# Adding layer outputs to the image by accumulating DMA instead of VectorE, in a four-layer image kernel

## The chip, the core and the metric

One core of a Trainium2 chip runs the kernel. Its engines each work through their own queue of instructions: TensorE (PE in the profile, its weight loads PEld), VectorE (DVE), ScalarE (ACT), GpSimd (POOL) and SyncE (SP), which here only issues DMAs. All data is float32. The metric is device time in microseconds, the median of several runs of the whole program.

## The reference

Four images `x[b]` of 256 channels and 64 x 64 pixels pass through four layers. Each layer normalises the image by groups, computes something from it and adds the result to the image.

```
x = x + L0(gn(x))   # xs = relu(gn1(conv3x3(x)));  attention over all 4096 pixels, y = softmax(theta^T phi) g
                    # L0 = 0.1 * gn2(w y) + xs
x = x + L1(gn(x))   # linear attention, 4 heads; output rms-normalised over channels
x = x + L2(gn(x))   # depthwise 3x3 and pointwise 1x1 convolution, weights generated from the image, + bias
x = x + L3(gn(x))   # 1x1 convolution with a mixture of 4 experts, mixed by the pooled image
```

Here `gn` is the plain group normalisation over 32 groups (8 channels each). A layer's group statistics need the whole image after the layer before.

## The kernel before

The 256 channels are two halves `h` of 128 partitions, and an image is `big[128, 2, 4096]`. `xp` is a padded copy of the image, `tpg` holds theta, phi and g of the attention. The rest are small buffers: `k4` (ten tiles of 128x1024, shared by all helpers), `k2` (six of 128x512) and `bank` (eight PSUM banks).

The helpers are Python generators. `convolve` (L306) is layer 0's 3x3 convolution; it ends by writing xs to DRAM (`xs_d`, L411). `project` and `attend` (L434) compute the attention; one turn of `attend` is one block of 256 by 512 logits. `tail` (L833) runs the rest for an image: `nonlocal_out` (L490, the end of layer 0), `linear_attention` (L541), `generated` (L675) and `mixed` (L776). Every `yield n` of these says how many turns of the partner the work just written is worth. `Chain` (L39) sums these values times a rate and gives one turn for each whole unit; `w.later(n, f)` has `f` written n turns later. Inside `manual_schedule` each engine's order is the order in which the turns write instructions.

The order of the work: convolution and projection of image 0; then, for b = 0 to 2, attention of image b interleaved with the tail of image b-1 and the convolution of image b+1 (rate 1.5 for b = 0, else 0.8), and the projection of image b+1. The end is written so:

```
attention, before = attend(B - 1), Chain(tail(B - 2, big, qT), 2.0).steps()
run(attention, before)
spare = ...
last = Chain(tail(B - 1, tpg[:, 0:NH, :], tpg[:, NH, :], in_turns(spare, k4))).steps()
run(last, before, before)
run(before)
```

So attention of image 3 runs with the tail of image 2 beside it, and what is left of that tail runs beside the tail of image 3, whose image lies in `tpg`. The first argument of `run` takes one turn, and each further argument takes one turn after it.

The additions that the change touches are all on VectorE: in `nonlocal_out` a chunk of xs and one of x are loaded (L517, L518), and two `scalar_tensor_tensor` on 128x1024 form the sum (L531, L533); in `linear_attention` L657 adds a scaled PSUM bank to the image; in `generated` L745 adds the pointwise product and the bias; in `mixed` L829 adds product and image into `res`, which L830 stores to `out`. After each of the first three, `bn_stats` reads the new chunk. The depthwise convolution is 8 `scalar_tensor_tensor` per half chunk (L760, "taps" below), 64 per image; the centre tap is ScalarE's (`centre`, L729), and the first half chunk has 8 more on VectorE that form the pointwise weights `pk` (L764). In the profile most VectorE operations carry the lines of two helpers: L93 (`tt`) and L96 (`stt`); the tile names tell them apart.

Of the kernel before, what the change touches and what calls it, by code (L numbers as in the profile page):

```python
# [38 lines left out]
class Chain:  # L39
# [5 lines left out]

    def later(self, n, f):

        self.due.append((max([n] + [k for k, _ in self.due]), f))

    def pending(self):  # L50
        while self.due:
# [2 lines left out]
    def steps(self):  # L54
        credit = 0.0
        for part in (self.layers, self.pending()):
            for n in part:
                credit += n * self.rate
                while credit >= 1:
                    credit -= 1  # L60
                    yield
                    self.due = [(k - 1, f) for k, f in self.due]
                    while self.due and self.due[0][0] <= 0:
                        self.due.pop(0)[1]()


@with_exitstack
def conv_preact_fast(ctx: ExitStack, tc: tile.TileContext, guard, x, wc, wtpg, ww, wqkv, wout, w1cat, wd2,
# [11 lines left out]
    def k4(name):  # L80
        return wk.tile([P, CH], F32, tag="k4", name=name, bufs=10)

    def k2(name):
        return wk.tile([P, 512], F32, tag="k2", name=name, bufs=6)

# [8 lines left out]

    def stt(o, a, s, b, op0, op1):
        nc.vector.scalar_tensor_tensor(o, a, s, b, op0, op1)  # L96


    xp = cp.tile([P, NH, HW + 2, HW], F32, name="xp")
# [123 lines left out]
    def stats_tile():  # L223
        return sp.tile([P, NH, 8, 6], F32, name="st")
# [80 lines left out]

    def convolve(w, b):  # L306

        st = stats_tile()
        for h in range(NH):
            for c in range(8):  # L310
# [81 lines left out]
        for i, (a, k) in enumerate(PRODUCTS):  # L392
            if k == 1:
                for op, *args in down(a):
                    op(*args)
                    yield 0.25
            v, u = across(k), us
            if i + 1 < len(PRODUCTS):
                us = load_filters(i + 1)
            w.later(1, lambda a=a, k=k, v=v, u=u: products(a, k, v, u))  # L400
            yield 0.9
        yield from w.pending()
        stats(3)
        bias = vec_s[:, V_SB, :]
# [2 lines left out]
        for c in range(N // CH):  # L407
            cols = bass.ts(c, CH)
            for h in range(NH):
                nc.scalar.activation(big[:, h, cols], big[:, h, cols], AF.Relu, bias=sh[:, h:h + 1], scale=sc[:, h:h + 1])  # L410
                w.later(1, lambda h=h, cols=cols: nc.sync.dma_start(out=xs_d[b, h, :, cols], in_=big[:, h, cols]))  # L411
                yield 0.3


# [75 lines left out]
    def nonlocal_out(w, b, big, k4):  # L490

        st = stats_tile()

        def load_y(c):
            yt = k4("yl")
            nc.sync.dma_start(out=yt, in_=y_d[b, :, bass.ts(c, CH)])
            return yt

        ys = [load_y(0), load_y(1)]
        for c in range(N // 512):  # L500
            cols = bass.ts(c, 512)
            if c % 2 == 0 and c // 2 + 2 < N // CH:
                ys.append(load_y(c // 2 + 2))
            for h in range(NH):
                ps = bank("ps_wy")
                nc.tensor.matmul(ps, ww_s[:, bass.ts(h, P)], ys[c // 2][:, bass.ts(c % 2, 512)], start=True, stop=True)  # L506
                nc.scalar.copy(big[:, h, cols], ps)
# [4 lines left out]
        PARTS = [(c, h) for c in range(N // CH) for h in range(NH)]  # L512

        def load_parts(i):
            c, h = PARTS[i]
            xs, xr = k4("xs"), k4("xr")
            nc.sync.dma_start(out=xs, in_=xs_d[b, h, :, bass.ts(c, CH)])  # L517
            nc.sync.dma_start(out=xr, in_=x[b, bass.ts(h, P), bass.ts(c, CH)])  # L518
            return xs, xr

        parts = [load_parts(0), load_parts(1)]
# [4 lines left out]
        for i, (c, h) in enumerate(PARTS):  # L526
            cols = bass.ts(c, CH)
            if i + 2 < len(PARTS):
                parts.append(load_parts(i + 2))
            xs, xr = parts[i]  # L530
            stt(xs, big[:, h, cols], sc[:, h:h + 1], xs, ALU.mult, ALU.add)  # L531
            yield 0.7
            stt(big[:, h, cols], xs, sh[:, h:h + 1], xr, ALU.add, ALU.add)  # L533
            yield 0.7
            for s in range(2):
                nc.vector.bn_stats(st[:, h, 2 * c + s, :], big[:, h, bass.ts(2 * c + s, 512)])
            yield 0.5
        return st


    def linear_attention(w, b, big, qT, k4, st):  # L541
# [108 lines left out]

        def added(c, z):
            cols = bass.ts(c, 512)
            for h in range(NH):
                pt = bank("ps_zt")
                for j in range(4):
                    nc.tensor.transpose(pt[:, bass.ts(j, P)], z[:, j, bass.ts(h, P)], ident)
                stt(big[:, h, cols], pt, gains[:, 1, h:h + 1], big[:, h, cols], ALU.mult, ALU.add)  # L657
                nc.vector.bn_stats(st[:, h, c, :], big[:, h, cols])

        last = None  # L660
        for c in range(NC):
            zb = outputs(c)
            yield 0.6
            if last is not None:
                added(c - 1, last)
            last = scaled(*zb)
            yield 0.6
        yield 1
        added(NC - 1, last)
        return st  # L670


# [2 lines left out]
    def generated(w, b, big, k4, st):  # L675
# [13 lines left out]
        nc.sync.dma_start(out=pk, in_=bp2)  # L689

        def load_wp2(j):
            t = k4("wp2").rearrange("p (r o) -> p r o", r=2)
            nc.sync.dma_start(out=t, in_=wp2[:, bass.ts(j, 2), :])
            return t

# [34 lines left out]
            return t  # L730

        def pointwise(c, s, dw):
            res = []
            for oh in range(NH):
                ps = bank("ps_pw")
                for h in range(NH):
                    nc.tensor.matmul(ps, pk[:, h * NH * P + oh * P:h * NH * P + (oh + 1) * P], dw[h][:, bass.ts(s, 512)],  # L737
                                     start=(h == 0), stop=(h == NH - 1))
                res.append(ps)
            w.later(1, lambda: pointwise_added(2 * c + s, res))  # L740

        def pointwise_added(c, res):
            cols = bass.ts(c, 512)
            for oh in range(NH):
                stt(big[:, oh, cols], res[oh], vec_s[:, V_L2B, oh:oh + 1], big[:, oh, cols], ALU.add, ALU.add)  # L745
                nc.vector.bn_stats(st[:, oh, c, :], big[:, oh, cols])

        ahead = centre(0)
        slices = [load_wp2(0), load_wp2(1)]
# [26 lines left out]
    def mixed(w, b, big, k4, st):  # L776
        ex = []
        for j in range(NE // 2):
            ex.append(k4("ex").rearrange("p (k o) -> p k o", k=2))
# [41 lines left out]
        nc.vector.tensor_copy(b3, pb3[:, 0:NH])  # L821
        for c in range(N // 512):
            cols = bass.ts(c, 512)
            for oh in range(NH):
                ps = bank("ps_ex")
                for h in range(NH):
                    nc.tensor.matmul(ps, wm[:, h, bass.ts(oh, P)], big[:, h, cols], start=(h == 0), stop=(h == NH - 1))  # L827
                res = k2("res")
                stt(res, ps, b3[:, oh:oh + 1], big[:, oh, cols], ALU.subtract, ALU.add)  # L829
                w.later(1, lambda oh=oh, cols=cols, res=res: nc.sync.dma_start(out=out[b, bass.ts(oh, P), cols], in_=res))  # L830
                yield 0.1

    def tail(b, big, qT, k4=k4):  # L833
        def layers(w):
# [637 lines left out]
```

## Time and profile before

| | |
|---|---|
| median of 3 runs | 3421.85 us (3421.0 to 3424.05) |
| the profiled execution | 3416.84 us |
| its span, first to last instruction | 3413.4 us |
| mean granted TensorE clock | 0.954 |
| TensorE busy | 3054.3 us, 89% of the span |
| VectorE busy | 2180.1 us, 64% |
| ScalarE busy | 1140.2 us, 33% |
| GpSimd busy | 96.4 us, 3% |
| DMA | 151.18 MB, mean 44 GB/s, all issued by SP |

A profile shows one execution. The page's slices cut the span into 40 equal parts of 85 us; a digit is the busy share in tenths. A group is one line, engine and shape: its instructions, their busy time and mean duration in ns, then how long the engine was idle just before them and which engine's instruction ended that. A busy TensorE can be one at a lowered clock; the granted clock stands beside it in the windows.

### The profile page before, as it was taken

To read this page: it belongs to the slowest core of one execution; us is meant where nothing else is said; L and a number is where in the kernel's file an instruction comes from. 1 tells how busy PE (TensorE), PEld (TensorE's weight loads), DVE (VectorE), ACT (ScalarE), POOL (GpSimd) and SP (SyncE) were. 2 spreads that over 40 slices of the span, in tenths; PEclk is the share of its full clock that TensorE was granted. 3 is DMA by queue.
4 is the path that set the end of the run, shared out by engine and by line. 5 is a ranking of instruction groups with operands and counts; after the bars stand their busy time and mean duration, and the time that the engine had idled before them with its cause. 6 is when DMAs were issued, how large, how long until landed. Compare 5 with 4: busy or idle time off the path is not lost.

```text
span 3413.4 us, 23977 instructions
## 1 busy us (share of the span) xinstructions
PE 3054.3 (89%) x8322; PEld 1470.1 (43%) x8322; DVE 2180.1 (64%) x2689; ACT 1140.2 (33%) x2115; POOL 96.4 (3%) x133
## 2 busy tenths in 40 slices
PE   3699999999999999999999999999999999738736
PEld 1254434445454444435454444445445553315412
DVE  8836674434636987873726996883653464794585
ACT  2033224333445322223445322213435434314210
POOL 0000000000000000000001000000000010000100
PEclk9899999999999999999999999999999999968867
DMA  5310001002101011112200011112200000210201
GB/s 197 100 50 23 30 25 53 6 4 81 49 0 31 4 68 68 40 46 88 67 1 25 9 65 59 41 33 77 77 28 3 4 7 31 77 49 13 77 12 50
DMA packets 78721, 151.18 MB, mean 44 GB/s; under 512 B 8320, under 2 KB 45952, under 8 KB 76416
## 3 DMA queue, kind: packets, MB, share of 16 engines
q1 hardware_dynamic: 78592, 149.56, 12.8%
q8 instruction: 68, 1.11, 0.1%
q14 instruction: 61, 0.50, 0.0%
HBM read 101.30 MB, written 48.23 MB: 44 GB/s over the span
## 4 chain that ended last, share of the span: by engine, by line
PE 71%; DVE 24%; issue 2%; ACT 2%; DMA 1%; POOL 0%; SPq 0%; DVEq 0%; ACTq 0%; POOLq 0%
PE pf L443 20%; PE py L473 19%; PE ps_conv L347 9%; DVE dw L96 6%; PE ps_qkv L574 5%; PE ps_tp L422 3%; PE ps_ex L827 3%; DVE tot L93 3%; DVE big L96 2%; PE ps_pw L737 2%; PE ps_wy L506 2%; PE ps_g L427 2%; PE ps_h L699 1%; PE ps_o L637 1%; DVE inv L457 1%
## 5 line engine op out<-in xcount | busy, mean ns | idle before, releaser
L444 ACT ACTIVATE pr<-pf 128x512 f32<-128x512 f32 x1024 | 602.3, 595 | 1221.4 <-PE pf L443 1173.3
L443 PE MATMUL pf<-tpg 128*128 128x512 f32 x2048 | 972.8, 597 | 5.8 <-DVE inv L457 3.5
L473 PE MATMUL py<-pr,tpg 128*128 128x512 f32 x2048 | 964.0, 593 | 7.1 <-ACT pr L444 7.1
L93 DVE TENSOR_TENSOR tot<-tot,pr 128x1024 f32<-128x1024 f32 x448 | 546.3, 1219 | 308.3 <-ACT pr L444 305.5
L473 PEld LDWEIGHTS py<-pr,tpg 128*128 128x128 f32 x2048 | 389.8, 191 | 500.0 <-issue 475.9
L443 PEld LDWEIGHTS pf<-tpg 128*128 128x128 f32 x2048 | 382.2, 191 | 457.4 <-issue 425.6
L347 PE MATMUL ps_conv<-v,u 128*128 128x512 f32 x768 | 354.9, 613 | 51.2 <-DVE v L93 28.2
L96 DVE SCALAR_TENSOR_TENSOR dw<-xp,dk,dw 128x1008 f32<-128x1008 f32 x224 | 283.5, 1267 | 7.1 <-ACT dw L729 3.6
L347 PEld LDWEIGHTS ps_conv<-v,u 128*128 128x128 f32 x768 | 150.1, 197 | 246.9 <-issue 206.3
L737 PE MATMUL ps_pw<-dw,pk 128*128 128x512 f32 x224 | 115.6, 650 | 66.8 <-DVE dw L96 66.8
L582 DVE TENSOR_REDUCE qs<-qk 128x16 f32<-128x512 f32 x24 | 16.5, 686 | 186.6 <-ACT qk L576 186.6
L574 PE MATMUL ps_qkv<-wqkv_s,xg 128*128 128x384 f32 x384 | 134.5, 498 | 0.0
L422 PE MATMUL ps_tp<-big,wtpg_s 128*128 128x512 f32 x256 | 117.7, 603 | 2.9 <-ACT big L410 2.9
L93 DVE TENSOR_TENSOR v<-ra 128x1024 f32<-128x1024 f32 x96 | 115.3, 1218 | 0.4
L93 DVE TENSOR_TENSOR tpg<-ps_g,bg_s 128x512 f32<-128x512 f32 x32 | 22.1, 691 | 144.9 <-PE ps_g L427 144.9
L457 DVE RECIPROCAL inv<-pss 128x512 f32<-128x512 f32 x32 | 107.3, 3352 | 7.2 <-PE pss L455 7.2
L737 PEld LDWEIGHTS ps_pw<-dw,pk 128*128 128x128 f32 x224 | 45.0, 208 | 131.8 <-DVE dw L96 71.3
L574 PEld LDWEIGHTS ps_qkv<-wqkv_s,xg 128*128 128x128 f32 x384 | 73.7, 197 | 51.0 <-issue 12.1
L171 POOL TENSOR_TENSOR rstd<-rstd,half 128x2 f32<-128x2 f32 x24 | 16.7, 697 | 2627.4 <-DVE rstd L247 2090.5
L423 ACT ACTIVATE tpg<-ps_tp,btp_s 128x512 f32<-128x512 f32 x64 | 43.8, 686 | 123.0 <-PE ps_tp L422 123.0
L576 ACT ACTIVATE qk<-ps_qkv,rinv 128x256 f32<-128x256 f32 x96 | 45.4, 473 | 116.6 <-PE ps_qkv L574 115.0
L827 PE MATMUL ps_ex<-big,wm 128*128 128x512 f32 x192 | 84.0, 593 | 0.0
(238 smaller groups left out, 2756.0 us busy)
## 6 DMA issues: line engine op xcount, KB each, us to landing
u<-filters SPq DMA_DIRECT2D x192, 128.0 KB, 2.3
xp<-in_x_dram SPq DMA_DIRECT2D x16, 1024.0 KB, 5.3
xs_d<-big SPq DMA_DIRECT2D x32, 512.0 KB, 2.8
xr<-in_x_dram SPq DMA_DIRECT2D x32, 512.0 KB, 4.5
out_dram<-res SPq DMA_DIRECT2D x64, 256.0 KB, 2.0
xs<-xs_d SPq DMA_DIRECT2D x24, 512.0 KB, 4.1
y_d<-yt SPq DMA_DIRECT2D x32, 256.0 KB, 2.0
yl<-y_d SPq DMA_DIRECT2D x14, 512.0 KB, 5.7
```

The lines of the kernel that those rows point to most:

```text
L93: nc.vector.tensor_tensor(o, a, b, op)
L96: nc.vector.scalar_tensor_tensor(o, a, s, b, op0, op1)
L347: nc.tensor.matmul(ps[oh], u[oh][:, h, :], v[:, bass.ts(h, 512)], start=(h == 0), stop=(h == NH - 1))
L422: nc.tensor.matmul(ps, wtpg_s[:, h, k, :], big[:, h, cols], start=(h == 0), stop=(h == NH - 1))
L427: nc.tensor.matmul(ps[:, j, :], big[:, h, bass.ts(4 * c + j, P)], wtpg_s[:, h, 2, :], start=(h == 0), stop=(h == NH - 1))
L443: nc.tensor.matmul(pf, phi[:, bass.ts(2 * m + s, P)], theta[:, bass.ts(q, 512)], start=True, stop=True)
L444: nc.scalar.activation(pr[:, bass.ts(s, 512)], pf, AF.Exp)
L457: nc.vector.reciprocal(inv, pss)
L473: nc.tensor.matmul(py, g[:, bass.ts(2 * m + s, P)], probs[i][:, bass.ts(s, 512)], start=(m == 0 and s == 0), stop=(m == NM - 1 and s == 1))
L574: nc.tensor.matmul(ps[:, 0:3 * HID], xg[:, h, bass.ts(j, P)], wqkv_s[:, h, :], start=(h == 0), stop=(h == NH - 1))
L737: nc.tensor.matmul(ps, pk[:, h * NH * P + oh * P:h * NH * P + (oh + 1) * P], dw[h][:, bass.ts(s, 512)], start=(h == 0), stop=(h == NH - 1))
L827: nc.tensor.matmul(ps, wm[:, h, bass.ts(oh, P)], big[:, h, cols], start=(h == 0), stop=(h == NH - 1))
```

## The change

Five sums become accumulating DMAs issued from GpSimd, `add_by_dma`. ScalarE first writes the term into an SBUF tile (or scales it in place in layer 0), and the DMA adds it to its destination. In layer 0, `xs_d` is filled with x before the convolution, xs is added to it in DRAM, and the sum is later added to the scaled output in SBUF; the loads of xs and x by chunk go. `bn_stats` of a chunk is written two turns after its DMA (one in layer 0). In layer 3 the sum is formed in the image and stored from there. `pool4` is the same allocator as `k4`, also where `k4` is handed in as alternating with spare tiles. `later` no longer keeps the order of earlier entries. Some yields change, and in the end phase the rate of image 2's tail is 3.0 with three turns per turn of the last tail.

```diff
 class Chain:
     def later(self, n, f):
-        self.due.append((max([n] + [k for k, _ in self.due]), f))
+        self.due.append((n, f))
...
+    def add_by_dma(o, i):
+        nc.gpsimd.dma_start(out=o, in_=i, accum_op=ALU.add)
...
     def convolve(w, b):
+        for h in range(NH):
+            nc.sync.dma_start(out=xs_d[b, h], in_=x[b, bass.ts(h, P), :])
...
-                    yield 0.25
+                    yield 0.3
...
-            yield 0.9
+            yield 1.1
...
-                w.later(1, lambda h=h, cols=cols: nc.sync.dma_start(out=xs_d[b, h, :, cols], in_=big[:, h, cols]))
+                w.later(1, lambda h=h, cols=cols: add_by_dma(xs_d[b, h, :, cols], big[:, h, cols]))
...  nonlocal_out
-            xs, xr = parts[i]
-            stt(xs, big[:, h, cols], sc[:, h:h + 1], xs, ALU.mult, ALU.add)
-            yield 0.7
-            stt(big[:, h, cols], xs, sh[:, h:h + 1], xr, ALU.add, ALU.add)
-            yield 0.7
-            for s in range(2):
-                nc.vector.bn_stats(st[:, h, 2 * c + s, :], big[:, h, bass.ts(2 * c + s, 512)])
-            yield 0.5
+                nc.scalar.activation(big[:, h, cols], big[:, h, cols], AF.Identity, bias=sh[:, h:h + 1], scale=sc[:, h:h + 1])
+                w.later(1, lambda h=h, cols=cols: add_by_dma(big[:, h, cols], xs_d[b, h, :, cols]))
+                w.later(2, lambda c=c, h=h: stats(c, h))
+                yield 0.7
+        yield from w.pending()
...  linear_attention, added
-                stt(big[:, h, cols], pt, gains[:, 1, h:h + 1], big[:, h, cols], ALU.mult, ALU.add)
-                nc.vector.bn_stats(st[:, h, c, :], big[:, h, cols])
+                nc.scalar.activation(o[:, h, :], pt, AF.Copy, scale=gains[:, 1, h:h + 1])
+            w.later(1, lambda: add_by_dma(big[:, :, cols], o))
+            w.later(3, lambda: stats(c))
...
-            yield 0.6      # twice per chunk
+            yield 0.5
...
+        yield from w.pending()
...  generated, pointwise
-                stt(big[:, oh, cols], res[oh], vec_s[:, V_L2B, oh:oh + 1], big[:, oh, cols], ALU.add, ALU.add)
-                nc.vector.bn_stats(st[:, oh, c, :], big[:, oh, cols])
+                nc.scalar.activation(o[:, oh, :], ps, AF.Identity, bias=vec_s[:, V_L2B, oh:oh + 1])
+            w.later(1, lambda: add_by_dma(big[:, :, cols], o))
+            w.later(3, lambda: stats(2 * c + s))
...  mixed
-                res = k2("res")
-                stt(res, ps, b3[:, oh:oh + 1], big[:, oh, cols], ALU.subtract, ALU.add)
-                w.later(1, lambda oh=oh, cols=cols, res=res: nc.sync.dma_start(out=out[b, bass.ts(oh, P), cols], in_=res))
-                yield 0.1
+                nc.scalar.activation(o[:, oh, :], ps, AF.Identity, bias=b3[:, oh:oh + 1])
+            w.later(1, lambda cols=cols, o=o: add_by_dma(big[:, :, cols], o))
+            w.later(3, lambda cols=cols: nc.sync.dma_start(out=to[:, :, cols], in_=big[:, :, cols]))
+            yield 0.3
...
-        attention, before = attend(B - 1), Chain(tail(B - 2, big, qT), 2.0).steps()
+        attention, before = attend(B - 1), Chain(tail(B - 2, big, qT), 3.0).steps()
...
-        run(last, before, before)
+        run(last, before, before, before)
```

More of the change, by code (lines that the diff above doesn't have):

```diff
@@ L61, in steps @@
                     yield
-                    self.due = [(k - 1, f) for k, f in self.due]
-                    while self.due and self.due[0][0] <= 0:
-                        self.due.pop(0)[1]()
+                    due = [(k - 1, f) for k, f in self.due]
+                    self.due = [d for d in due if d[0] > 0]
+                    for k, f in due:
+                        if k <= 0:
+                            f()
 @with_exitstack
@@ L81, in k4 @@
         return wk.tile([P, CH], F32, tag="k4", name=name, bufs=10)
+    pool4 = k4
     def k2(name):
@@ L510, in nonlocal_out @@
                 nc.vector.bn_stats(st[:, h, c, :], big[:, h, cols])
[L512 to L521, printed above, removed]
         bias = vec_s[:, V_WB, :]
@@ L525, in nonlocal_out, with stats @@
         st = stats_tile()
[L526 to L529, printed above, removed]
-            xs, xr = parts[i]
-            stt(xs, big[:, h, cols], sc[:, h:h + 1], xs, ALU.mult, ALU.add)
-            yield 0.7
-            stt(big[:, h, cols], xs, sh[:, h:h + 1], xr, ALU.add, ALU.add)
-            yield 0.7
+        def stats(c, h):
             for s in range(2):
                 nc.vector.bn_stats(st[:, h, 2 * c + s, :], big[:, h, bass.ts(2 * c + s, 512)])
-            yield 0.5
+        for c in range(N // CH):
+            cols = bass.ts(c, CH)
+            for h in range(NH):
+                nc.scalar.activation(big[:, h, cols], big[:, h, cols], AF.Identity, bias=sh[:, h:h + 1], scale=sc[:, h:h + 1])
[3 more added lines that the diff above has]
+        yield from w.pending()
         return st
@@ L652, in added @@
             cols = bass.ts(c, 512)
+            o = pool4("o").rearrange("p (h n) -> p h n", h=NH)
             for h in range(NH):
@@ L656, in added, with stats @@
                     nc.tensor.transpose(pt[:, bass.ts(j, P)], z[:, j, bass.ts(h, P)], ident)
-                stt(big[:, h, cols], pt, gains[:, 1, h:h + 1], big[:, h, cols], ALU.mult, ALU.add)
-                nc.vector.bn_stats(st[:, h, c, :], big[:, h, cols])
+                nc.scalar.activation(o[:, h, :], pt, AF.Copy, scale=gains[:, 1, h:h + 1])
+            w.later(1, lambda: add_by_dma(big[:, :, cols], o))
+            w.later(3, lambda: stats(c))
+        def stats(c):
+            for h in range(NH):
+                nc.vector.bn_stats(st[:, h, c, :], big[:, h, bass.ts(c, 512)])
         last = None
@@ L666, in linear_attention @@
             last = scaled(*zb)
-            yield 0.6
+            yield 0.5
         yield 1
         added(NC - 1, last)
+        yield from w.pending()
         return st
@@ L691, in load_wp2 @@
         def load_wp2(j):
-            t = k4("wp2").rearrange("p (r o) -> p r o", r=2)
+            t = pool4("wp2").rearrange("p (r o) -> p r o", r=2)
             nc.sync.dma_start(out=t, in_=wp2[:, bass.ts(j, 2), :])
@@ L732, in pointwise @@
         def pointwise(c, s, dw):
-            res = []
+            cols = bass.ts(2 * c + s, 512)
+            o = pool4("o").rearrange("p (h n) -> p h n", h=NH)
             for oh in range(NH):
@@ L738, in pointwise, with stats @@
                                      start=(h == 0), stop=(h == NH - 1))
[L739 to L743, printed above, removed]
+                nc.scalar.activation(o[:, oh, :], ps, AF.Identity, bias=vec_s[:, V_L2B, oh:oh + 1])
+            w.later(1, lambda: add_by_dma(big[:, :, cols], o))
+            w.later(3, lambda: stats(2 * c + s))
+        def stats(c):
             for oh in range(NH):
-                stt(big[:, oh, cols], res[oh], vec_s[:, V_L2B, oh:oh + 1], big[:, oh, cols], ALU.add, ALU.add)
-                nc.vector.bn_stats(st[:, oh, c, :], big[:, oh, cols])
+                nc.vector.bn_stats(st[:, oh, c, :], big[:, oh, bass.ts(c, 512)])
         ahead = centre(0)
@@ L778, in mixed @@
         for j in range(NE // 2):
-            ex.append(k4("ex").rearrange("p (k o) -> p k o", k=2))
+            ex.append(pool4("ex").rearrange("p (k o) -> p k o", k=2))
             nc.sync.dma_start(out=ex[j], in_=experts[:, bass.ts(j, 2), :])
@@ L820, in mixed @@
         b3 = sp.tile([P, NH], F32, name="b3")
-        nc.vector.tensor_copy(b3, pb3[:, 0:NH])
+        nc.vector.tensor_scalar(b3, pb3[:, 0:NH], -1.0, None, ALU.mult)
+        to = out[b].rearrange("(h p) n -> p h n", h=NH)
         for c in range(N // 512):
             cols = bass.ts(c, 512)
+            o = pool4("o").rearrange("p (h n) -> p h n", h=NH)
             for oh in range(NH):
```

## The prediction

> **What bounds the kernel now.** I read the page's busy times and slices first, to see which engine is full and where.
>
> ```profile
> PE 3054.3 (89%) x8322; PEld 1470.1 (43%) x8322; DVE 2180.1 (64%) x2689; ACT 1140.2 (33%) x2115; POOL 96.4 (3%) x133
> ...
> PE   3699999999999999999999999999999999738736
> DVE  8836674434636987873726996883653464794585
> ```
>
> TensorE is full from slice 3 to slice 34, the four attention phases; VectorE is not. Work taken from VectorE there is hidden already. Windows over 255 to 2890 us, 85 us each, leave TensorE idle for only 75 us. Only the last six slices and the first two have TensorE waiting. So I cut the end into windows (columns: stretch, its length, then busy us and instructions of PE, PEld, DVE, ACT, POOL, then granted clock, DMA share, GB/s).
>
> ```profile
> 2383.00:2943.00 560.00, 559.20 (x1544) 268.10 (x1543) 296.41 (x358) 243.50 (x474) 26.45 (x27) 1.00 0.07 23
> 2943.00:2970.00 27.00, 17.40 (x36) 7.74 (x37) 19.40 (x24) 11.76 (x20) 0.00 (x0) 0.81 0.68 242
> 2970.00:3063.00 93.00, 27.10 (x53) 11.80 (x52) 87.16 (x111) 8.70 (x10) 1.39 (x2) 0.61 0.15 45
> 3063.00:3145.00 82.00, 70.77 (x284) 49.92 (x283) 37.65 (x57) 41.83 (x89) 9.78 (x16) 0.88 0.04 14
> 3145.00:3230.00 85.00, 64.41 (x240) 39.42 (x238) 57.03 (x111) 16.39 (x68) 9.46 (x10) 0.90 0.21 78
> 3230.00:3250.00 20.00, 17.09 (x38) 3.77 (x38) 0.95 (x6) 14.56 (x24) 0.35 (x1) 0.84 0.00 1
> 3250.00:3365.00 115.00, 41.99 (x64) 15.62 (x64) 107.51 (x108) 8.54 (x8) 0.00 (x0) 0.61 0.03 9
> 3377.00:3413.40 36.40, 29.37 (x66) 12.80 (x66) 12.32 (x18) 0.00 (x0) 0.00 (x0) 0.92 0.30 118
> ```
>
> The last attention (to 2943) is TensorE alone. Then two stretches are VectorE: 2970 to 3063 (image 3's residual sums beside image 2's depthwise taps) and 3250 to 3365 (image 3's taps). Between them image 3's linear attention is TensorE and waits; the last 36 us are TensorE's. The chain of waits dates the stages:
>
> ```profile
> 2952.60 15.93 PE ps_wy L506 x32
> ...
> 3064.00 5.28 PE ps_qkv L574 x16
> ...
> 3231.03 6.20 PE ps_h L699 x8
> ...
> 3376.95 29.05 PE ps_ex L827 x64
> ```
>
> **What is removed and added.** The groups by form price both sides:
>
> ```profile
> L96 DVE SCALAR_TENSOR_TENSOR big<-ps_pw,vec_s,big 128x512 f32<-128x512 f32 x48 | 35.5, 740 | 0.3 <-PE ps_pw L737 0.2
> ...
> L96 DVE SCALAR_TENSOR_TENSOR big<-xs,sh,xr 128x1024 f32<-128x1024 f32 x24 | 30.7, 1280 | 0.3
> L96 DVE SCALAR_TENSOR_TENSOR xs<-big,sc,xs 128x1024 f32<-128x1024 f32 x24 | 30.6, 1275 | 0.0
> ...
> L507 ACT COPY big<-ps_wy 128x512 f32<-128x512 f32 x48 | 28.1, 585 | 33.5 <-PE ps_wy L506 33.5
> ```
>
> Per image VectorE loses 16 sums of 1.28 us (20.4) and 48 of 0.74 (35.6): 56 us. ScalarE gains 8 x 1.23 (the 128x1024 row of L410) and 48 x 0.59: 38 us, on an engine that is a third busy. 40 accumulating DMAs of 512 KB go to GpSimd's queue, ahead of later rsqrt steps (L171); SP loses 16 loads and 8 stores of 512 KB, and gets two 2 MB copies x to xs_d ahead of the filter loads; out stores become 8 of 512 KB, which now wait on SP for the sum to land.
>
> The trace has no accumulating DMA; its time per 512 KB, call it t, decides much. The nearest rows are plain copies:
>
> ```profile
> 4.00:16.00 12.00, 0.00 (x0) 0.00 (x0) 9.96 (x21) 0.00 (x0) 0.00 (x0) 1.00 1.02 434
> ...
> xs<-xs_d SPq DMA_DIRECT2D x24, 512.0 KB, 4.1
> ```
>
> At the 434 GB/s of that window 512 KB take 1.2 us, the lower end; with no overlap at all, one landing (4.1) plus about 0.9 to issue, 5.0 us, the upper end. Both operands must be read, so I take two passes, t = 2.5 us, and for one DMA from issue to landing 6 us (the load's 4.1 and most of a 2.8 us store).
>
> The Trainium skill, "Collectives: The Full Stack", section "The bandwidth ceiling", says that an add in the DMA path costs its second read and not the arithmetic, about half the copy rate; no row here shows it. By it t would be 2.4.
>
> A rule speaks against the change. Waits of GpSimd on VectorE's port would show in its own small steps: the same power operation means 697 ns on rstd and 1234 on zr, which is twice as wide: at most 0.5 us for a step. The skill, "SBUF — State Buffer", section "SBUF: two separate sides", says that a DMA issued from GpSimd cannot get its descriptors written while VectorE runs an operation in a two-port mode. By it each of the 16 accumulations on the end's path (8 in stage A, 8 in E below) could lose one VectorE operation of about 1.2 us, 19 us together; the operations beside them are two-input ones, so I take nothing.
>
> **New waits and who stands behind them.** On VectorE each `bn_stats` waits for a DMA; behind it stand the `tot` sums of the attention, which free the `pr` tiles of `k4`, which ScalarE and so TensorE need. With a turn of 3.4 us and ten tiles a delay of some three turns is covered, and one or two turns are what a landing of 6 us costs. On GpSimd each DMA waits for ScalarE's term, written a turn earlier; behind it stand the rsqrt steps of linear attention, whose results scale the next chunk. On SP the stores of `out` wait for their sums; behind them stand the filter loads of the next convolution, some ten units later, and the convolution's first write of `big` must wait for those stores: 45 us in phases 1 and 2 against 8 x (2.5 + 1.2) = 30. All three are priced at nothing while t is near 2.5; if the cover is gone, VectorE's delay comes through on TensorE, 8 us per layer for each us of t.
>
> **What moves.** Counting the yields: attention 3 gives 130 turns. At rate 2.0 image 2's chain gets through 65 units of its 108, which ends 14 taps into the depthwise part; at 3.0 it gets through 43 of 98 (the new yields are smaller), which ends just before the first tap. So 14 taps (1.27) and 8 pk sums (0.745), 24 us of VectorE, move into the end. Image 2's ps_h matmuls stay in attention 3, so TensorE's 559 us there stay. In the end both chains go one unit per turn, as before.
>
> **The end, stage by stage** (before, 470 us from 2943).
>
> A, to image 3's first ps_qkv (3064). Image 3's scale is ready at 2985. Instead of 16 sums woven with 34 taps, eight ScalarE steps of 1.23 us feed eight DMAs: 8 x 2.5 = 20, then some 2 us of landing tail: 3007. Statistics 1.4, then the 15 us which lie between bn_aggr (3049) and 3064: 3023. Minus 41. The deferred taps don't hold it: 13 taps and 8 pk are 22 us in this time.
>
> B, linear attention to 3227. Image 2's 27 us of ps_ex leave; about 14 us of its ps_pw come. VectorE holds 44 taps (55 us), 44 of the layer's own and some 7 of statistics, 106 of about 160 us. At the end the last sum has to land before its statistics, plus 8. Net minus 4.
>
> C, ps_h of image 3: 7 us of image 2's ps_pw in the same TensorE queue, part of it in gaps: plus 4.
>
> D, image 3's taps (was 114). VectorE loses six chunk pairs of sums (9 us), gains image 2's layer 3 weights and finish (6). But image 2's ps_ex (27 us on TensorE, evicted by ScalarE) starts about 17 us after the first tap, and the centre tap of part 2 (L729, 1.15) is queued on ScalarE behind its evictions: ready near 48 us, while VectorE has work to 32. Plus 16. The last sum's landing before the last statistics: plus 6. Net plus 19.
>
> E, last layer (36): per chunk 3.4 us of TensorE against 2.5 + 1.2 for sum and store, so 30 us, then one landing and a larger store: plus 8.
>
> A to E: -41 - 4 + 4 + 19 + 8 = -14.
>
> **The attention phases.** Convolution gets 31 instead of 27 turns in phases 1 and 2 (1.1 for 0.9) and 73 for 64 chain turns in phase 0; TensorE's idle time there, 11.5, 7.7 and 5.9 us plus 10 of lowered clock, is mostly late v tiles of VectorE: I take back 15 of 35. From layer 0's first scaled chunk to the TensorE step of the next group statistics (pm) I count 8 turns of 3.4 us (8 matmuls), 27 us, against 8 x 2.5 + 3 = 23 for the sums: nothing, but beyond t = 3.0 each phase pays 8 us per us of t, twice. At the start the 4 MB copy goes ahead of the filter stores, which land well before the first matmul at 55: plus 3. Sum minus 12.
>
> Total -26: the profiled execution (span 3413.4, time 3416.8) becomes 3391. The median of the runs lies 5 us above that execution: 3396, stated as 3395.
>
> With t = 5.0: A +20, E +20, phases +32: 46 us slower, 3468. With t = 1.2: A is held by ScalarE's eight steps, -48, and E gives +6: 35 us faster, 3387. The sign changes near t = 3.6.
>
> **Rivals.**
> Slower: the accumulating DMA moves 512 KB in over 3.6 us. Then stage A, the last layer and the PE step after layer 0 in phases 1 and 2 wait on it; at 5.0 it is 3468, and with a landing of 10 us at each of five boundaries some 10 more. For it: no such DMA is in the trace, and lone landings are 4.1. Against: 434 GB/s in the same engines.
> Much faster: the end follows VectorE's sum. It falls from 328 to 328 - 80 + 24 = 272 us; if the whole 57 is saved and the phases give 12, 3348 + 5 = 3353. For it: 87 of 93 and 107 of 115 busy. Against: stages B and E are not VectorE's, and the centre tap stalls it.
> Nothing moves: A's 41 us come back in C, D and E and the phases give nothing: 3415 to 3429. For it: the sums above nearly cancel.
> That it does not do what it says is partly so already: by the count only taps move.
>
> **How the numbers follow.** Forecast case (t 2 to 3.3) 0.47, slow DMA 0.29, end follows VectorE 0.12, nothing moves 0.12. Two runs of this kernel differ by up to 0.1%, so 0.2% (7 us) is what can be told apart. Faster: 0.47 + 0.12 = 0.59, with a little given to same: 0.58; same 0.13; slower 0.29. The range reaches from inside the much-faster case to the slow DMA's end: 3340 to 3478. The likeliest case alone: 3376 (no stall on the centre tap) to 3412 (t = 3.3).
>
> **What would show it.** Right: DMA rows big<-xs_d and big<-o whose stream gives near 2.5 us per 512 KB; first ps_qkv of the last image about 80 us after the last attention, not 121; a 10 to 20 us VectorE wait on the centre tap (ScalarE) early in the last taps; res and xs rows gone. Wrong: those DMAs at over 4 us each with bn_stats waiting on DMA in every layer; pm matmuls waiting after layer 0 in phases 1 and 2; GpSimd busy for microseconds per DMA, or rsqrt late behind it; the attention phases over 560 us.

## The result, and the profile after

The changed kernel takes 3437.4 us (median of 4 runs, 3432.3 to 3444.7) beside 3421.5 us for the kernel before on the same chip: a ratio of 1.0047, with an interval of 1.0027 to 1.0066. It is slower by about 16 us; the forecast was 26 us faster. The profiled execution has a span of 3437.5 us, 24 more than before.

The page of the changed kernel (busy us, share of the span, instructions; then the slices) shows VectorE relieved as planned and TensorE no less busy:

```profile
PE 3057.7 (89%) x8322; PEld 1481.6 (43%) x8322; DVE 1968.4 (57%) x2433; ACT 1301.5 (38%) x2339; POOL 279.2 (8%) x293
...
PE   3689989999899999999899999999999999577545
...
DVE  8836665433446966783435975783543354555662
```

VectorE lost 212 us, about the 4 x 56 that were counted. The slices say where that did not help: TensorE's last six read 5 7 7 5 4 5 where they read 7 3 8 7 3 6, and a few of its nines have become eights. The page's DMA list (bytes of one, median us from issue to landing) has the new transfers:

```profile
big<-o POOLq DMA_DIRECT2D x72, 512.0 KB, 5.7
...
xs_d<-big POOLq DMA_DIRECT2D x32, 512.0 KB, 11.6
big<-xs_d POOLq DMA_DIRECT2D x24, 512.0 KB, 8.7
```

I cut the profiled executions at the same events: the first ps_tp, the first ps_tp of image 3, the last pf, then image 3's first ps_qkv, last ps_zt, first ps_h, last ps_pw and first ps_ex. All lengths are in us. In the last column the ratio to the kernel before is that of the timed runs; 0.001 is 3.4 us. One profile stands for each kernel. The same instructions in the three phases differ by up to 7 us between executions (2155.9 to 2162.6 in the changed kernel, `rate2`, `centre_ahead` and `turns4`), and 26 runs of the kernel before on one chip span 3412.0 to 3428.0 us, 0.47%, where the prediction took 0.1%.

| kernel | start | 3 phases | att. 3 | to qkv | to zt | to ps_h | to pw | to ex | end | ratio |
|---|---|---|---|---|---|---|---|---|---|---|
| before | 179.9 | 2160.6 | 597.5 | 125.9 | 160.3 | 6.7 | 132.3 | 13.6 | 36.6 | 1 |
| changed | 186.6 | 2161.7 | 594.0 | 92.1 | 154.4 | 17.0 | 165.4 | 19.9 | 46.4 | 1.0047 |
| l0_only | 182.9 | 2169.6 | 603.4 | 93.7 | 163.1 | 6.7 | 132.3 | 13.5 | 40.7 | 0.9948 |
| rate2 | 186.9 | 2155.9 | 603.4 | 85.5 | 151.8 | 28.0 | 133.2 | 19.8 | 46.3 | 0.9987 |
| move_only | 180.4 | 2157.3 | 573.2 | 113.5 | 159.0 | 13.0 | 173.2 | 13.6 | 37.0 | 1.0027 |
| centre_ahead | 188.3 | 2162.6 | 593.9 | 91.9 | 151.6 | 17.0 | 165.0 | 19.9 | 46.4 | 1.0047 |
| turns4 | 187.0 | 2155.9 | 594.0 | 104.7 | 149.5 | 44.0 | 133.3 | 19.9 | 46.3 | 1.0060 |
| no_l2 | 187.2 | 2161.4 | 593.9 | 92.9 | 143.2 | 17.0 | 157.3 | 13.8 | 46.7 | 0.9994 |
| no_l3 | 186.3 | 2144.9 | 594.0 | 91.9 | 153.3 | 17.0 | 176.4 | 19.9 | 37.9 | 1.0026 |
| old_pace | 182.2 | 2145.8 | 594.0 | 92.6 | 151.4 | 17.0 | 164.8 | 19.9 | 46.3 | 1.0004 |
| l0_pace | 187.0 | 2181.5 | 603.3 | 91.7 | 163.2 | 6.7 | 132.3 | 13.5 | 40.1 | 1.0024 |
| l0_pace_spread | 185.2 | 2171.0 | 603.4 | 91.7 | 160.5 | 6.7 | 134.7 | 13.4 | 41.5 | 0.9968 |
| l0_rate15 | 181.5 | 2162.5 | 623.1 | 101.8 | 127.4 | 6.7 | 134.2 | 13.5 | 37.8 | 0.9923 |
| l0_late_pm | 179.7 | 2165.7 | 621.2 | 103.7 | 123.3 | 6.7 | 131.4 | 13.8 | 38.8 | 0.9920 |
| l0_rate12 | 182.0 | 2162.0 | 664.9 | 71.7 | 126.5 | 6.7 | 133.7 | 13.5 | 37.7 | 0.9961 |
| all_mended | 181.2 | 2148.9 | 618.2 | 115.8 | 121.5 | 14.3 | 133.4 | 19.8 | 46.3 | 0.9955 |
| l0_rate15_spread | 171.3 | 2169.2 | 623.1 | 101.3 | 127.4 | 6.7 | 134.2 | 13.5 | 37.8 | 0.9907 |

The changed row against the first: the stretch to image 3's first ps_qkv is 34 us shorter, as forecast; from its last ps_zt on all four stretches are longer (10 + 33 + 6 + 10); the start loses 7. The windows of the two middle stretches of the changed kernel, and of the stretch from ps_h to ps_pw before (busy us and instructions of PE, PEld, DVE, ACT, POOL, granted clock, DMA share, GB/s):

```profile
3189.00:3205.80 16.80, 1.45 (x10) 1.17 (x10) 15.78 (x26) 0.76 (x2) 1.92 (x2) 0.50 0.46 131
3205.80:3371.20 165.40, 96.47 (x200) 37.88 (x197) 105.69 (x119) 47.37 (x69) 21.17 (x18) 0.72 0.39 86
```

```profile
3230.90:3363.20 132.30, 58.33 (x101) 19.25 (x100) 106.67 (x109) 23.10 (x32) 0.00 (x0) 0.64 0.02 8
```

VectorE does the same 106 us in both, but needs 165 instead of 132 for it: it waits, while TensorE does 38 us more, image 2's. VectorE's waits from 3189 us on (us in all, times, longest) name what for:

```profile
DVE st L752 <- DMA tpg<-o: 24.9, 7, 11.4
DVE st L752 <- DMA big<-o: 17.4, 2, 14.9
DVE rt L100 <- ACT rt L735: 16.5, 2, 15.3
```

That is 42 us before statistics whose sum hadn't landed and the forecast 15 us on the centre tap. The longest wait for each image's sums stands ahead of image 3's first tap (image 2's sum) and ahead of its last bn_aggr (image 3's) (VectorE's timeline, then GpSimd's with the issue of those two sums):

```profile
3224.26 1.29 DVE L752 BATCH_NORM_STATS2 st<-big 128x6 f32<-128x512 f32 x2 [14.93 <-DMA big<-o]
...
3374.25 1.29 DVE L752 BATCH_NORM_STATS2 st<-tpg 128x6 f32<-128x512 f32 x2 [11.39 <-DMA tpg<-o]
```

```profile
3218.38 1.23 POOL L103 DMA_DIRECT2D big<-o  x1 [13.15 <-ACT o L746]
...
3369.35 1.20 POOL L103 DMA_DIRECT2D tpg<-o  x1 [22.08 <-ACT o L746]
```

So the DMA itself is only the end of these waits, 5.9 of the 14.9 us and 4.9 of the 11.4. Before that the sum waits for its term: the first one's product is on TensorE at 3213.65, behind twelve of image 3's ps_h, and then ScalarE evicts it.

### The profile page after: what moved, and what is told of

Same layout as the page of the kernel before. It is cut to its first block, busy times and chain, and to the rows that moved or that the text cites. A ratio compares the mean times of both kernels' runs of the same rounds, so it can differ in the third digit from the quotient of the medians.

```text
span 3437.5 us, 24114 instructions
## 1 busy us (share of the span) xinstructions
PE 3057.7 (89%) x8322; PEld 1481.6 (43%) x8322; DVE 1968.4 (57%) x2433; ACT 1301.5 (38%) x2339; POOL 279.2 (8%) x293
## 4 chain that ended last, share of the span: by engine, by line
PE 77%; issue 12%; DVE 6%; DMA 2%; ACT 2%; POOL 1%; SPq 0%; POOLq 0%; ACTq 0%; DVEq 0%
PE pf L452 23%; PE py L482 23%; PE ps_conv L356 8%; PE ps_qkv L573 5%; PE ps_tp L431 3%; PE ps_pw L744 3%; PE ps_ex L835 2%; PE ps_g L436 2%; PE ps_o L636 2%; DVE dw L100 2%; PE ps_wy L515 1%; PE ps_h L705 1%; PE ps_ctx L593 1%; PE ps_zt L656 1%; PE pss L464 1%
## 5 line engine op out<-in xcount | busy, mean ns | idle before, releaser
L356 PE MATMUL ps_conv<-v,u 128*128 128x512 f32 x768 | 362.4, 623 | 79.8 <-issue 50.2
L103 POOL DMA_DIRECT2D big<-o x72 | 87.4, 1226 | 568.3 <-ACT o L746 403.2
L359 ACT COPY one<-ps_conv 128x512 f32<-128x512 f32 x48 | 28.1, 585 | 217.1 <-PE ps_conv L356 214.8
L746 ACT ACTIVATE o<-ps_pw,vec_s 128x512 f32<-128x512 f32 x64 | 43.9, 686 | 169.7 <-PE ps_pw L744 129.5
```

The costliest lines, as they stand in the source:

```text
L103: nc.gpsimd.dma_start(out=o, in_=i, accum_op=ALU.add)
L356: nc.tensor.matmul(ps[oh], u[oh][:, h, :], v[:, bass.ts(h, 512)], start=(h == 0), stop=(h == NH - 1))
```

## The experiments

**Is it the DMA, the move, or both together?** Three kernels split the change. `l0_only` is the kernel before with layer 0's part of the change alone; `rate2` is the changed kernel with the old end phase; `move_only` is the kernel before with the new one.

```diff
 l0_only, on the kernel before: the prefill of xs_d, add_by_dma to xs_d, and in nonlocal_out
-            stt(xs, ...); yield 0.7; stt(big, ...); yield 0.7; bn_stats; yield 0.5
+            nc.scalar.activation(big[:, h, cols], ..., AF.Identity, bias=sh, scale=sc)
+            w.later(1, lambda: add_by_dma(big[:, h, cols], xs_d[b, h, :, cols]))
+            yield 0.7
+            if i >= 2: stats(*PARTS[i - 2])
 rate2, on the changed kernel
-  Chain(tail(B - 2, big, qT), 3.0) ... run(last, before, before, before)
+  Chain(tail(B - 2, big, qT), 2.0) ... run(last, before, before)
 move_only, on the kernel before: the same two lines the other way
```

> The kernel before with layer 0 alone by accumulating DMA (x copied to xs_d ahead, xs added to it in DRAM, the sum added to the scaled output; statistics two chunks later); layers 1 to 3 on VectorE, rate 2.0 and two turns as before. Theory (the DMAs cost what was forecast, 2.5 us per 512 KB, and the loss lies in layers 1 to 3 and in the move): image 3's first ps_qkv comes 33 us earlier after the last attention, as in the changed kernel; the start loses 7; the nine units fewer in layer 0 let 14 more taps of image 2 pass in attention 3: 3385 to 3402. Rival 1 (accumulating DMAs cost wherever they stand, in the start and beside the attention): 3421 or more. Rival 2 (the 33 us come back later, since VectorE's taps or the centre tap hold the end anyway): 3412 to 3425.

Measured 0.9948 (0.9931 to 0.9965), 3403 us: the upper edge of the theory's range. The stretch to ps_qkv is 32 us shorter. The taps up to ps_ex are as long as before, so the second rival falls; 7 us come back elsewhere in the end (3 in the linear attention, 4 in the last layer). The start has +3, attention 3 +6, with 16 more of image 2's ps_pw in it, and the phases +9, hardly more than executions differ: of the first rival a part remains (layer 0's statistics, below).

> The changed kernel with the old rate 2.0 and two turns of image 2's tail per turn of the last one. By count 27 taps and 8 pk sums of image 2 then lie in attention 3 that the changed kernel has in the end, and image 2's layer 3 ends before image 3's taps begin. Theory (what is lost after image 3's linear attention is image 2's deferred work in the same queues: its pointwise product ahead of ps_h, its layer 3 ahead of the centre tap): 13 of stage C and 15 of stage D return, 3400 to 3420. Rival 1 (the landings at the layers' last chunks are the loss, whoever stands beside them): 3430 to 3440. Rival 2 (attention 3 becomes VectorE's with more of the taps in it): 3440 or more, and attention 3 longer than 560 us.

Measured 0.9987 (0.9975 to 1.0000), so the move costs the changed kernel about 20 us. The stretch from ps_h to ps_pw is back at 133. But the end of the linear attention got worse, 28 us to ps_h instead of 17, where the theory had 13 us return: there rival 1 is right. The timeline of `rate2` just there (start, length, engine, instruction, idle time before it and what ended it):

```profile
3178.99 19.25 SPq L838 DMA_DIRECT2D out_dram<-big  x5
...
3183.97 1.20 POOL L103 DMA_DIRECT2D big<-o  x1 [2.23 <-ACT o L836]
3184.70 2.94 POOL L103 DMA_DIRECT2D tpg<-o  x2
...
3201.89 1.29 DVE L663 BATCH_NORM_STATS2 st<-tpg 128x6 f32<-128x512 f32 x2 [13.25 <-DMA tpg<-o]
3206.01 1.29 DVE L663 BATCH_NORM_STATS2 st<-tpg 128x6 f32<-128x512 f32 x2 [2.84 <-DMA tpg<-o]
```

Image 3's last two sums (tpg<-o) are issued at 3184.7 and 3185.9 behind image 2's layer 3: its sums (big<-o) and its stores (out_dram). They land at 3202 and 3206, 17 and 20 us later; between 3170 and 3206 the DMA engines move 247 GB/s on average. Landing alone takes 4.9 us, as four of image 3's sums in the changed kernel show, issued between 3147 and 3162 us with nothing else under way:

```profile
DMA to landing us min/median/max: 4.9/4.9/4.9
```

> The kernel before with rate 3.0 and three turns, sums on VectorE as before. By count it then leaves all 64 taps, 8 pk sums and the 8 ps_h of image 2 to the end (before: 50 taps), and image 2's layer 3 ends at image 3's first taps. Theory (the deferred work meets image 3's queues): 15 to 30 us slower than the kernel before, 3436 to 3452. Rival (the move is harmless, the DMAs are the loss): 3417 to 3426.

Measured 1.0027 (1.0014 to 1.0040), 9 us slower: the theory's sign, below its size. The stretch from ps_h to ps_pw is 41 us longer; attention 3 gives 24 back, since all of image 2's ps_h left it. So the move loses time with no accumulating DMA anywhere.

**What stretches image 3's taps?** The forecast said: the centre tap behind image 2's evictions on ScalarE. `centre_ahead` takes that wait away; `turns4` puts all of image 2's layer 3 ahead of image 3's taps.

```diff
 centre_ahead, on the changed kernel, for image 3
-        ahead = centre(0)            # centre(i + 1) is written in part i
+        ahead = [centre(0), centre(1)]   # centre(i + 2) is written in part i
 turns4, on the changed kernel
-        run(last, before, before, before)
+        run(last, before, before, before, before)
```

> The changed kernel with image 3's centre taps written two half chunks ahead instead of one, so that the second is in ScalarE's queue before image 2's layer 3 evictions. Theory: the one wait of 15 us of the taps on the centre tap goes, and stage D shortens by 10 to 15 us: 3422 to 3428. Rival (VectorE's taps then wait for the next thing, the landings that the last statistics need or image 2's layer 3): 3433 to 3440.

Measured 1.0047 (1.0032 to 1.0063): nothing gained. VectorE's timeline has the wait of the changed kernel first, and then what stands in its place:

```profile
3282.26 7.81 DVE L100 SCALAR_TENSOR_TENSOR rt<-xp,dk,rt 128x1008 f32<-128x1008 f32 x6 [15.29 <-ACT rt L735]
```

```profile
3293.54 1.29 DVE L752 BATCH_NORM_STATS2 st<-tpg 128x6 f32<-128x512 f32 x2 [19.44 <-DMA tpg<-o]
```

The second centre tap is ready, the taps run on, and then the statistics of the first chunk wait 19 us for a sum whose product stood behind image 2's ps_ex on TensorE, and whose DMA stood behind the last of image 2's eight sums and its stores: 10 us pass before its issue at 3284.2 and 9.3 from there to its landing. One queue was cleared, the next one held.

> The changed kernel with four turns of image 2's tail for each turn of the last tail, rate 3.0 as changed. By count image 2's layer 3 ends at turn 171 and image 3's taps begin at 177; in the changed kernel at 185 and 177. Theory (what stretches image 3's taps is image 2's layer 3 in the same queues): the stretch from image 3's ps_h to its last ps_pw falls from 165 to 132 to 140 us, image 3's linear attention gets 10 to 20 longer, in all 10 to 20 us faster than the changed kernel: 0.999 to 1.002 of the kernel before. Rival (the sum of the work left to the end decides, wherever it falls): 1.003 to 1.006.

Measured 1.0060 (1.0046 to 1.0074): the rival. The stretch from ps_h to ps_pw falls to 133, as the theory said, and the same time turns up just ahead of it, 44 us to ps_h:

```profile
3220.27 0.16 DVE L245 COPY gm<-pm 128x2 f32<-128x2 f32 x1 [17.89 <-PE pm L243]
3230.80 0.16 DVE L254 TENSOR_SCALAR rstd<-pv 128x2 f32<-128x2 f32 x1 [9.78 <-PE pv L252]
```

Image 3's small steps of the group statistics now stand behind image 2's ps_ex on TensorE. In these two runs what is left of image 2 costs the end phase its time wherever it falls.

**Which layer's sums?** `no_l2` and `no_l3` put the sums of one layer back on VectorE in the changed kernel, with the lines of the kernel before.

> The changed kernel with layer 2's pointwise sums back on VectorE, as before; all else as changed. Theory (statistics wait for landings at the end of each image's layer 2): image 2's wait of 14.9 us before image 3's first tap and image 3's of 11.4 us before bn_aggr go, and the three of 3 to 4 us between; VectorE gets 16 sums of 0.74 us back among image 3's taps: 10 to 20 us faster than the changed kernel, 0.999 to 1.002 of the kernel before. Rival (the sums on VectorE cost what the landings did): 1.004 to 1.006.

Measured 0.9994 (0.9985 to 1.0003), 18 us faster than changed. The 14.9 us wait and the one before bn_aggr go (to pw -8, to ex -6), and so do 11 us in the linear attention, where image 2's pointwise sums run.

> The changed kernel with layer 3's sums back on VectorE and its stores by half chunk, as before; all else as changed. Theory (image 2's eight accumulations and eight stores of layer 3 stand in the DMA queues ahead of image 3's first pointwise sums, and the last layer of image 3 waits for its own sums to land): the last layer gets 8 to 10 us shorter, and in image 3's taps the wait for the centre tap or for the landing, 15 to 19 us, falls by 8 to 15: 1.000 of the kernel before, 0.998 to 1.002. Rival (only the last layer's end gains): 1.002 to 1.003. Rival (nothing): 1.0047.

Measured 1.0026 (1.0017 to 1.0035), 7 us faster, but not where the theory put it. The last layer gets 8.5 us shorter, and the taps 11 longer, for image 2's sums are VectorE's again (117 us busy there instead of 106). VectorE's wait for the centre tap is down to 1.2 us in all, and again the stretch is no shorter for it. The three phases are 17 us shorter in the profile, more than such executions differ; of that the change in layer 3's yields, which shifts the convolution's turns, is a possible cause that no run isolates.

**The pace of the convolution.** The forecast took 15 us from the new yields (0.3 and 1.1). `l0_pace` adds them to `l0_only`; `old_pace` takes them out of the changed kernel; `l0_pace_spread` tests why.

```diff
 l0_pace, on l0_only (old_pace: the other way, on the changed kernel)
-                    yield 0.25
+                    yield 0.3
-            yield 0.9
+            yield 1.1
 l0_pace_spread, on l0_pace
-                    w.later(1, lambda oh=oh, t=dst[oh]: rows_joined(a, oh, t))
+                    w.later(1 + oh, lambda oh=oh, t=dst[oh]: rows_joined(a, oh, t))
```

> Layer 0 alone by accumulating DMA, with the convolution's new yields (0.3 for 0.25, 1.1 for 0.9) added. The forecast took back 15 us of TensorE's idle time in the attention phases from them. By that theory 8 to 15 us faster than layer 0 alone, so about 0.991 to 0.993 of the kernel before. Rival (v tiles were not late for want of turns, and the first convolution, which runs without an attention beside it, gets longer by the 7 us that the changed kernel shows there): 0.995 to 0.998.

Measured 1.0024 (1.0015 to 1.0033): 26 us slower than without them, beyond the rival. The two profiles differ by 13: the start takes 4 us more and the phases 12, the rest 3 less. Two waits of ps_conv in phase 1 are new (engine and line, what it waited for, us in all, times, longest; "issue" means that the profile shows nothing it waited for):

```profile
PE ps_conv L351 <- DVE inv L461: 5.9, 1, 5.9
PE ps_conv L351 <- issue: 4.4, 1, 4.4
```

In `l0_only` ps_conv waits 0.2 us there.

> The changed kernel with the convolution's old yields (0.25 and 0.9). Theory (the new yields lose time instead of gaining the forecast's 15 us, as they did beside layer 0 alone, by 22 us): 12 to 25 us faster than the changed kernel, 0.998 to 1.001 of the kernel before, with the start 3 to 4 us shorter and the waits of ps_conv in phases 1 and 2 gone. Rival (the loss beside layer 0 alone came from where its turns happened to fall): 1.003 to 1.005.

Measured 1.0004 (0.9994 to 1.0015), 15 us faster than the changed kernel: the theory. The gain lies in the phases (-16) and the start (-4). The changed kernel's timeline in phase 1, where the yields act (VectorE's row sums write `big` and `both`, then comes the v tile that TensorE waits for; the attention's lines between are left out):

```profile
1497.93 1.22 DVE L97 TENSOR_TENSOR both<-big,t 128x1024 f32<-128x1024 f32 x1
...
1502.60 2.48 DVE L100 SCALAR_TENSOR_TENSOR big<-big 128x1024 f32<-128x1024 f32 x2
...
1504.99 1.22 DVE L97 TENSOR_TENSOR both<-big,t 128x1024 f32<-128x1024 f32 x1
...
1509.66 2.48 DVE L100 SCALAR_TENSOR_TENSOR big<-big 128x1024 f32<-128x1024 f32 x2
1512.05 1.22 DVE L97 TENSOR_TENSOR v<-ra 128x1024 f32<-128x1024 f32 x1
...
1513.37 2.90 PE L356 MATMUL ps_conv<-v,u 128*128 128x512 f32 x3 [7.14 <-issue]
```

Twelve row sums, both halves, are written in one turn, ahead of v: 14 us of VectorE where a turn has 3.4. The profile names nothing for TensorE's wait of 7.1 us, but it ends 0.1 us after v is written. In `old_pace` the same twelve also stand in one run (to 1487 us); over the three phases ps_conv waits 25 us there, 37 in the changed kernel and 18 before.

> Layer 0 alone with the new yields, and the second half's row sums (rows_joined) one turn after the first half's. Theory (the new yields put both halves' row sums, up to 12 operations of 1.2 us, ahead of a v tile in one turn, and TensorE waits for it): the waits of 4.4 and 5.9 us of ps_conv in phase 1 go, 8 to 15 us faster than with the yields alone, 0.998 to 1.000 of the kernel before. Rival (the burst isn't what makes v late; the turns come too far apart from the chain's needs): 1.001 to 1.004.

Measured 0.9968 (0.9957 to 0.9978): 19 us faster than `l0_pace` by the timed runs, 11 by the profile. So most of what the new yields cost beside layer 0 is this burst. One wait of 6.3 us remains in phase 1.

**Versions that beat both kernels.** `l0_rate15` is `l0_only` with less of image 2 left to the end and the copy of image 0 after the first filters; the next three vary it. `all_mended` is the changed kernel with every repair found so far.

```diff
 l0_rate15, on l0_only
-  Chain(tail(B - 2, big, qT), 2.0)
+  Chain(tail(B - 2, big, qT), 1.5)          # l0_rate12: 1.25
+            if b == 0 and i == 8: fill()    # x[0] to xs_d, written after the first filters
 l0_late_pm, on l0_rate15: after layer 0's last bn_stats, and in linear_attention
+        if b < B - 1: yield 2.4
-            yield 0.6      # twice per chunk
+            yield 0.5
 l0_rate15_spread, on l0_rate15: w.later(1 + oh, ...) for rows_joined
 all_mended, on the changed kernel: old yields, 1.5, two turns, fill() late, yield 2.4
```

> Layer 0 alone by accumulating DMA, with rate 1.5 instead of 2.0 for image 2's tail in attention 3, and the copy of image 0 from x to xs_d issued after the ninth product's filters instead of ahead of all filters. By count all but one of image 2's 36 taps that were left to the end lie in attention 3. Theory: the start's 3 us return (first product at 55 us, not 58), attention 3 takes some 10 us more for the pointwise products, the last stages lose image 2's taps, sums and most of its layer 3, 15 to 20 us: 0.990 to 0.994 of the kernel before. Rival (attention 3 is held up by VectorE with the taps in it): 0.996 to 1.000.

Measured 0.9923 (0.9910 to 0.9937). Attention 3 takes 20 us more than in `l0_only` and what follows 29 less: 36 less in the linear attention, which has its queues nearly to itself, and 8 more ahead of it. The first ps_conv starts at 55.1 us again and not at 58.1, though by the trace only one 2 MB half of the copy moved, from 35.0 to 51.4 us; the other is issued at 22.5 us in both.

> Layer 0 alone by accumulating DMA with the late copy of image 0, and rate 1.25 instead of 1.5, so that by count all of image 2's tail ends six turns before the last attention does. Theory (what is left of image 2 costs more in the end, where it meets image 3's queues, than on TensorE in attention 3): attention 3 longer by its layer 3, 20 to 27 us, the stretch to image 3's first ps_qkv shorter by 10 to 15 and its linear attention by 5 to 15: 0.989 to 0.993 of the kernel before. Rival (attention 3 is TensorE's alone, each us moved there is paid there): 0.995 to 0.998.

Measured 0.9961 (0.9948 to 0.9975), the rival: attention 3 takes another 42 us, the end only 32 less. Best among the three rates tried is 1.5.

> The kernel with layer 0 alone by accumulating DMA, rate 1.5 and the late copy of image 0, with 2.4 units more between layer 0's statistics and the TensorE step that needs them (pm), for images 0 to 2; the yields of the linear attention's output are 0.5 for 0.6, as in the changed kernel. Theory (in phases 1 and 2 TensorE waits 6.5 us for the landed sums and then runs some 80 us at a lowered clock): those waits fall under 2 us, each phase gets 4 to 8 us shorter, 0.988 to 0.990 of the kernel before. Rival (the turns given there are missed later, by the convolution): 0.991 to 0.994.

Measured 0.9920 (0.9905 to 0.9934): no gain. The wait did not shrink; VectorE, which waits for the landings first, seems to be late by as much, which no run isolates. TensorE's timeline:

```profile
874.86 0.59 PE L238 MATMUL pm<-mv,avg 128*128 128x2 f32 x2 [5.95 <-DVE mv L233]
```

> The changed kernel, all four layers by accumulating DMA, with the old yields, rate 1.5 and two turns, the late copy of image 0 and pm after layer 0 later by 2.4 units. Theory (with image 2 out of the way what is left of the loss are the landings at the ends of layers 1, 2 and 3, 10, 6 and 9 us of TensorE's or VectorE's time on image 3's path, against 9 us of shorter linear attention): 8 to 18 us slower than layer 0 alone so mended, 0.992 to 0.995 of the kernel before. Rival (the sums' DMAs cost nothing once image 2's don't stand ahead of them): 0.990 or less.

Measured 0.9955 (0.9940 to 0.9969): the theory, at its upper edge. The sums of layers 1 to 3 by DMA still cost 11 us beside `l0_rate15`: +8 to ps_h, +6 to ps_ex, +8.5 in the last layer and +14 to ps_qkv, where image 2's layer 3 and image 3's layer 0 share the DMA queues, against 14 us in the phases and 6 in the linear attention.

> Layer 0 alone by accumulating DMA at rate 1.5 and with the late copy of image 0, and the second half's row sums one turn after the first half's, with the old yields. Theory (the burst of row sums makes a v tile late with the old yields too): 4 to 10 us faster than without, 0.989 to 0.991 of the kernel before. Rival (with the old yields the burst is covered): 0.992 to 0.994.

Measured 0.9907 (0.9891 to 0.9922), the fastest of all, some 32 us below the kernel before. The intervals of it and of `l0_rate15` overlap. What it gains is the start, 171 for 181 us, where no attention covers the burst; the phases gain nothing, which fits the rival there: beside an attention the old yields cover it. Its page shows TensorE with fewer idle slices at the end than either kernel:

```profile
PE 3064.6 (91%) x8322; PEld 1481.5 (44%) x8322; DVE 2107.0 (62%) x2625; ACT 1177.7 (35%) x2147; POOL 151.7 (4%) x197
...
PE   3799999999899999999899999999999999977736
```

## Why the prediction was wrong, step by step

The forecast was -26; the two profiled spans differ by +24, the medians by +16. By its own terms, in the profiled executions:

- **The price of the DMA held.** t was taken as 2.5 us per 512 KB. Two windows in stage A, where the stream runs without a gap, give 197 and 207 GB/s, 2.7 and 2.5 us:

```profile
2992.00:3004.00 12.00, 0.00 (x0) 0.00 (x0) 7.00 (x10) 6.76 (x7) 4.48 (x6) 0.50 1.04 197
3004.00:3012.00 8.00, 0.00 (x0) 0.00 (x0) 7.96 (x10) 0.00 (x0) 0.00 (x0) 0.50 1.05 207
```

  Against the plain 434 GB/s of before this is just under half. The Trainium skill, "Collectives: The Full Stack", section "The bandwidth ceiling", says that an add in the DMA path costs a second read, about half the copy rate. The half agrees; that the second read is the reason no run shows. A lone landing was taken as 6; it is 4.9 from SBUF and 6.7 for the first one from DRAM. The slow-DMA rival is out, and so is its reading of a slower result.
- **Waits of GpSimd on VectorE** were taken as nothing. In stage A each issue holds GpSimd 0.86 to 0.92 us while VectorE adds, and the first sum lands 6.7 us after its issue: of the 19 us that the prediction worked out from the skill's page "SBUF — State Buffer", section "SBUF: two separate sides", the half in A does not show, as the prediction took it for two-input operations. In E VectorE is busy for 0.3 of 46 us, so E tests nothing.
- **A (-41) was nearly right: -34** in the changed kernel, -32 in `l0_only`. The largest step of the mechanism held.
- **E (+8): +9.8**, and 8.5 of it go in `no_l3`.
- **B, C and D (-4 + 4 + 19 = +19) failed: +44.** Cut at the prediction's own ends (image 3's pm at 3227, its pooled step at 3249) B is +2, C +12, D +30. The forecast priced one landing at each layer's end, 6 to 8 us, as if that DMA were alone, and the meeting of the two images as one wait, on the centre tap. The size of that wait was right (15.3 for 16), but taking it away gained nothing (`centre_ahead`). In its place stood the other queues: VectorE waited 25 us in D for image 3's sums, where 6 was priced, and in C TensorE did 7.1 us of image 2's ps_pw and waited 2.2 us for image 2's statistics, where 4 was priced. Two terms were missing, and the runs give their size in the changed kernel: the work of image 2 left to the end (`rate2` gives 20 us back) and layer 2's sums by DMA (`no_l2`, 18). They may overlap, since no run takes both away. The move's own price was 22 us of VectorE's taps that "don't hold" A, and TensorE's 27 us less in B against 14 and 7 more; `move_only` shows it to lose 9 us net.
- **The attention phases (-12) failed: +4** (+7 at the start, +1, -3.5). The -15 was credited to the new yields, which lose 15 us in the changed kernel and 26 beside layer 0. That `old_pace`, without them, has -15 in the phases and +2 at the start is a match by chance; where its -15 comes from no run isolates. "More turns" was read as more cover; the twelve row sums of one turn were not looked at.
- **Layer 0's statistics, priced at nothing** (27 us of TensorE's work against 23 for the sums), do wait, once in each of phases 1 and 2: 6.5 and 5.7 us in the changed kernel. TensorE got through its part in 22 us, and the first landing alone is 6.6 to 6.7. In `l0_only`:

```profile
875.80 0.59 PE L238 MATMUL pm<-mv,avg 128*128 128x2 f32 x2 [6.81 <-DVE mv L233]
```

  The 80 us around it, in `l0_only` and then in the kernel before (columns as above), are granted a clock of 0.91 against 1.00, with 7.5 us less of TensorE:

```profile
823.00:903.00 80.00, 70.45 (x186) 34.56 (x185) 38.34 (x68) 41.67 (x66) 11.01 (x14) 0.91 0.28 53
```

```profile
813.00:893.00 80.00, 77.95 (x188) 34.72 (x186) 61.66 (x87) 32.30 (x55) 1.39 (x2) 1.00 0.30 92
```

The rival "nothing moves" (0.12) had the mechanism nearest to what happened: A's gain comes back in C, D and E, and the phases give nothing. More came back than that rival allowed (3415 to 3429). The two failed sums are 25 and 16 us; with 7 in A and 2 in E they make up the 50 us between the forecast's sum and the profile.

## What to carry to other kernels

A sum moved to a DMA pays where VectorE holds the chain, as in image 3's layer 0 (32 to 34 us). It is dear where VectorE was not the limit and the statistics need the last chunk: price its landing behind what another image has in the same queues, and with the product and the eviction ahead of it, not alone. Before a stall is costed, ask what the waiting engine meets next if that stall is taken away; where two chains share the queues, as here, count the work left to the shared stretch: moving it about inside that stretch gained nothing. Yields given as cover move bursts as well: count what the fullest turn holds on each engine.

## What the runs showed of the hardware

An accumulating DMA streams at 197 to 207 GB/s, out of DRAM into SBUF as here; its issue holds GpSimd 0.86 us for 128 x 1024 and 1.2 us for 128 x 2 x 512. From issue to landing 512 KB take 4.9 us alone, SBUF to SBUF, 6.6 to 6.7 for the first of a stream out of DRAM, and 17 to 20 behind another image's sums and stores (`rate2`). A copy of 2 MB from DRAM to DRAM delays small transfers issued behind it: with its second half issued at 35.0 us in `l0_only`, the 256 KB filter stores behind it took up to 7.7 us to land, against 2.5 to 3.3 before, and the first convolution started at 58 us instead of 55.
